# SyncE takes over 71 gathered rows of a deformable convolution, fetching each position by itself

## The chip, the core and the metric

The kernel runs on one core of one Trainium2 chip. The metric is device time in microseconds (us) of one execution. The engines are TensorE (PE; its weight loads are PEld), VectorE (DVE), ScalarE (ACT), GpSimd (POOL) and SyncE (SP); sixteen DMA engines move data between HBM and the on-chip memory.

## The reference, cut to what matters

The input x is (4, 128, 128, 128): four images, 128 channels, 128 x 128 pixels. Layer 0 is a deformable 3 x 3 convolution and a mixture of 8 experts; layer 1 is a Fourier mixing and a routed network of 64 experts. The change lies in the sampling of the deformable convolution:

```python
offset = _offset_conv(x, w_off)
...
py = base_y.astype(x.dtype)[None] + dy
px = base_x.astype(x.dtype)[None] + dx
sampled = _bilinear_gather(x, py, px)
O = w_conv.shape[0]
return jnp.einsum('bckhw,ock->bohw', sampled, w_conv.reshape(O, C, K * K))
```

For each output pixel and each of the nine taps k, a position is computed from the data, the four pixels around it are read over all 128 channels, weighted bilinearly and summed. Everything after it (the expert layer, the mixing, the routing) is done per group of image rows as soon as its nine taps are there.

## The kernel before, in words

**Tables.** Each image is normalised and written to HBM as a table of 129 x 130 entries of 256 floats: an entry holds a pixel and the pixel below it. Two entries in a row, 2 KB, are the four corners of one position. `positions` (line 649) computes for each pixel and tap the entry's number into `im.index` (128 partitions = the x of the pixel, then y, then tap) and the four corner weights.

**Chunks.** An image's 128 rows are worked in 32 groups of four rows (`row_groups`, line 162), and a group in nine chunks, one per tap; 4 x 288 = 1152 chunks in all. For one chunk (class `Chunk`, line 751):
- `gather` issues four indirect DMAs on GpSimd, one for each image row: each reads 128 positions of 2 KB, one into each partition, into a quarter of the tile g (six such tiles).
- `weighted` multiplies three of the rows by their weights on VectorE; `weighted_too` does the fourth row on ScalarE, four instructions (in a group's first chunk, tap 0, VectorE does all four rows).
- `summed` transposes and adds the four corners on TensorE, 16 matmuls into the bank trg.
- `moved` copies the result to sT on ScalarE, and `convolved` multiplies it by the weights of its tap, into sums.

**Order.** Every instruction is issued in an order written by hand (the helper at line 104, which is why most of the profile stands on L104). Time is counted in turns, two half-chunks to a chunk: the main loop makes for step n the weighting of chunk n+1, the sums of chunk n, the move of chunk n-1, and then issues the gathers of a chunk `AHEAD` = 6 steps further on (`in_turn`, line 1587). Between these, small jobs written as generators (tables of the next image, the expert layer of the last group, routing) take their turns. An engine's instructions run in that order, and an instruction that waits holds up all behind it on its engine.

**SyncE** issues the plain DMAs in the same hand-written order: loads of image blocks (xc), stores of table blocks (table<-ent), loads of the rows of a group (xg), stores of layer 1's input (x_d), expert weights and, at the end, the output. Each of its DMAs counts on one of eight completion counters, used in turn, so a DMA waits for the one issued eight before it.

**Pads.** Four padded tiles, pads 0 to 3 (line 332), hold blocks of four image rows with a zero border, for the offset convolution: `padding` (line 456) fills them on ScalarE and `offsets` (line 465) reads them in matmuls. A block uses two, and successive blocks alternate between the pairs. Late in the kernel all four serve as rooms for expert weights (`flat_pads`, line 335; `rooms`, line 1652).

**Stages.** First the table of image 0 (no gathers yet); then the sampling of all images, with the next image's table made beside it and, in the last image, the routed experts of the first three; then an ending for the last image's experts. `turns.hop` is 1 in the first and last stage and 3 during sampling.

Of the kernel before, what the change touches and what calls it, by code (L numbers as in the profile page):

```python
# [42 lines left out]
F32 = mybir.dt.float32  # L43
I32 = mybir.dt.int32
U32 = mybir.dt.uint32
AF = mybir.ActivationFunctionType
ALU = mybir.AluOpType
AX = mybir.AxisListType
# [3 lines left out]
P = 128  # L52
# [5 lines left out]
HID = 512  # L58
# [6 lines left out]
TAPS = 9  # L65
EPS_C = 1e-6
EPS_T = 1e-5
RB = 8
CB = 16
TW = P + 1  # L70
TC = P + 2
# [14 lines left out]
BANKS = 6  # L86
AFTER = 11
SPACE = 13
BLOCK = 84
FILL = "fill"  # L90
DONE = "done"
# [98 lines left out]
def metaformer_kernel(  # L190
# [50 lines left out]
    with ExitStack() as main:  # L241
# [91 lines left out]
        for pad in pads:  # L333
            nc.vector.memset(pad, 0.0)
        flat_pads = [pad.rearrange("p y x -> p (y x)")[:, 0:HID].unsqueeze(1) for pad in pads]
        aT_sb = wts.tile([P, P], F32, name="aT_sb")

        gwT_sb = wts.tile([P, 2 * E1], F32, name="gwT_sb")
# [126 lines left out]
        def offsets(im, t, padded):  # L465
# [8 lines left out]
            for k in range(3):  # L474
                for h in range(2):
                    eng.tensor.matmul(
                        po[h * P // 2 : (h + 1) * P // 2],
                        lhsT=woff_sb[:, k, :],
                        rhs=pads[(2 * t + h) % 4][:, :, k : k + P],
                        start=(k == 0),  # L480
                        stop=(k == 2),
                    )
# [268 lines left out]
        class Chunk:  # L751


            def __init__(self, group, k):
                self.group, self.k = group, k
                self.shared = k > 0

            def gather(self):
                self.g = pg.tile([P, 4, 4, P], F32, name="g", tag="g")
                im = self.group.im  # L760
                for s, y in enumerate(self.group.rows):
                    eng.gpsimd.indirect_dma_start(
                        out=self.g[:, s].rearrange("p v c -> p (v c)"),
                        out_offset=None,
                        in_=im.table,
                        in_offset=bass.IndirectOffsetOnAxis(
                            ap=im.index[:, y, self.k : self.k + 1], axis=0
                        ),
                    )

            def weighted(self):
                n = 3 if self.shared else 4
# [4 lines left out]
                )  # L777

            def weighted_too(self):
                g, y = self.g[:, 3], self.group.rows[3]  # L780
                w = self.group.im.weight[y // CB]
                for v in range(4):
                    eng.scalar.activation(
                        g[:, v, :], g[:, v, :], AF.Copy, scale=w[:, y % CB, self.k, v : v + 1]
                    )

            def summed(self):

                self.tr = bank([P, 4, P], "trg")
                for s in range(4):  # L790
                    for v in range(4):
                        eng.tensor.matmul(
                            self.tr[:, s, :],
                            lhsT=self.g[:, s, v, :],
                            rhs=ident,
                            is_transpose=True,
                            start=(v == 0),
                            stop=(v == 3),
                        )

            def moved(self):
# [2 lines left out]
                eng.scalar.copy(group.sT[self.k], self.tr)  # L804
                turns.start(group.convolved(self.k))


        exps = []

# [776 lines left out]

        def in_turn():

            for b in range(NB):
                for number, (rows_of, minus, runs) in enumerate(orders[b]):  # L1590
                    im = images[b]
                    if im.sent <= P // RB or not im.weight.keys() >= {y // CB for y in rows_of}:
                        raise ValueError("a table is late")
                    group = Group(images[b], number, rows_of, minus, runs)
                    group.begin()
                    for k in range(TAPS):
                        chunk = Chunk(group, k)
                        chunk.gather()
                        yield chunk

        source = in_turn()
        chunk = [next(source) for _ in range(AHEAD)]
        turns.hop = HOP
# [14 lines left out]
        while n < total + 3 or turns.jobs:  # L1618
# [134 lines left out]
```

## Time and profile before

| | |
|---|---|
| three runs, median | 6126.47 us (6125.08 to 6129.46) |
| the profiled execution | 6137.75 us, its span 6135.8 us |
| granted TensorE clock, mean | 0.953 |
| indirect DMAs for the tables | 4608, 3.8 us from issue to landing at the median |
| first and last of them start | 120.9 us, 5932.9 us |
| HBM read, written | 1381.43 MB, 136.85 MB |
| software queue (the gathers) | 64.9% of the sixteen DMA engines' time |
| SyncE's queue | 14.1% of it |

The page gives each engine's busy time as a share of the span, then groups of instructions by line, engine and operation with the idle time before them and what ended it ("issue": nothing that the profile shows was waited for). SyncE's instructions only issue, wait or set registers, so it has no busy share; its queue is asked for by tile.

### The profile page before, as it was taken

Reading aid. Unit: us, or ns where it says so; the run is one execution under the profiler, and the core shown is the slowest. Engines: PE = TensorE matmul, PEld = TensorE weight load, DVE = VectorE, ACT = ScalarE, POOL = GpSimd, SP = SyncE. Lnnn points to the kernel's source line nnn. Section 1 sums busy time; section 2 is a strip of 40 time slices with the busy share of each in tenths; the row PEclk is TensorE's granted clock in tenths of the full one; section 3 lists DMA queues with packets and bytes.
Section 4 is the critical chain, followed back from the end, with each engine's and each line's share of the span. In section 5 each row is a group of like instructions: output and inputs, shape, how many; then the busy total and the mean of one; then the engine's idle time right before and its main releaser. Section 6 shows DMA issues by size and latency. Waiting matters only on the chain.

```text
span 6135.8 us, 103694 instructions
## 1 busy us (share of the span) xinstructions
PE 5429.9 (88%) x31399; PEld 3754.5 (61%) x31399; DVE 4849.1 (79%) x15411; ACT 3880.8 (63%) x10047; POOL 4477.5 (73%) x4801
## 2 busy tenths in 40 slices
PE   6889999998899999998899999898888998999884
PEld 3566666666656666666666666666655665666653
DVE  5688888887788888887778888888788777788872
ACT  4567667675666766666666676666655665666662
POOL 5777777777777777777777777777777777777750
PEclk8999999999999999999999999999999999999996
DMA  7778787877777777877777778778777897999777
GB/s 233 227 238 252 243 253 240 254 236 224 240 241 243 244 244 246 246 237 221 235 245 244 245 237 248 241 237 252 221 226 215 291 337 216 328 336 318 223 221 269
DMA packets 579180, 1525.24 MB, mean 249 GB/s; under 512 B 86456, under 2 KB 225408, under 8 KB 578624
## 3 DMA queue, kind: packets, MB, share of 16 engines
q0 software_dynamic: 369664, 1210.35, 64.9%
q1 hardware_dynamic: 206656, 299.87, 14.1%
q10 hardware_dynamic: 2304, 8.39, 0.3%
q8 instruction: 253, 4.15, 0.3%
q14 instruction: 303, 2.48, 0.1%
HBM read 1381.43 MB, written 136.85 MB: 247 GB/s over the span
## 4 chain that ended last, share of the span: by engine, by line
DMA 26%; PE 25%; DVE 21%; issue 10%; POOL 9%; ACT 9%; DVEq 0%; POOLq 0%; ACTq 0%; SPq 0%
DMA g<-table,index 24%; POOL g L104 9%; PE trg L104 8%; DVE x L104 7%; DVE g L104 7%; PE sums L104 6%; PE pe L104 4%; ACT g L104 3%; PE po L104 2%; PE tr L104 2%; ACT xn L104 1%; ACT L104 1%; ACT sT L104 1%; PE small L104 1%; DVE a_st L104 1%
## 5 line engine op out<-in xcount | busy, mean ns | idle before, releaser
L104 POOL DMA_INDIRECT g<-table,index x4608 | 4375.2, 949 | 1413.2 <-issue 977.9
L104 DVE TENSOR_TENSOR g<-g,small 128x1536 f32<-128x1536 f32 (+1 forms) x1152 | 2082.6, 1808 | 827.5 <-DMA g<-table,index 762.8
L104 PEld LDWEIGHTS trg<-ident,g 128*128 128x128 f32 x18432 | 2113.8, 143 | 679.5 <-issue 458.4
L104 PE MATMUL trg<-ident,g 128*128 128x128 f32 x18432 | 2251.1, 276 | 120.7 <-DVE g L104 51.5
L104 ACT ACTIVATE g<-g,weight 128x128 f32<-128x128 f32 x4096 | 1305.9, 391 | 820.0 <-DMA g<-table,index 811.2
L104 DVE SCALAR_TENSOR_TENSOR x<-pe,gate,x 128x128 f32<-128x128 f32 x4064 | 1381.5, 342 | 97.9 <-PE pe L104 43.8
L104 PE MATMUL sums<-sT,wconv_sb 128*128 128x512 f32 x2304 | 1209.8, 626 | 42.2 <-ACT sT L104 41.5
L104 PE MATMUL pe<-ew_sb,nT 128*128 128x512 f32 x2048 | 1042.8, 607 | 76.6 <-ACT sT L104 42.1
L104 PEld LDWEIGHTS sums<-sT,wconv_sb 128*128 128x128 f32 x2304 | 437.4, 202 | 520.2 <-issue 431.8
L104 ACT COPY sT<-trg 128x512 f32<-128x512 f32 x1152 | 654.5, 568 | 135.9 <-PE trg L104 134.9
L104 PEld LDWEIGHTS pe<-ew_sb,nT 128*128 128x128 f32 x2048 | 328.9, 193 | 242.4 <-issue 104.1
L104 ACT ACT_TABLE_LOAD x264 | 338.7, 1283 | 13.5 <-DVE nmax L104 8.1
L104 ACT ACTIVATE tn<-x,d_nb,d_rs 128x128 f32<-128x128 f32 x512 | 210.9, 483 | 199.0 <-DVE d_nb L104 198.7
L104 ACT ACTIVATE c_rs<-c_mv,eps_c 128x4 f32<-128x4 f32 x128 | 38.1, 297 | 359.3 <-DVE c_mv L104 325.6
L104 ACT ACTIVATE n<-x,b_nb,b_rs 128x128 f32<-128x128 f32 x512 | 210.2, 481 | 83.6 <-DVE b_nb L104 72.1
L104 PE MATMUL tr<-ident,whole 128*128 128x128 f32 x512 | 92.2, 308 | 165.3 <-ACT whole L104 158.4
L104 ACT ACTIVATE xn<-x,c_nb,c_rs 128x128 f32<-128x128 f32 x512 | 211.3, 487 | 9.5 <-DVE c_nb L104 7.6
L104 PE MATMUL po<-pad,woff_sb 128*64 128x512 f32 x768 | 214.6, 678 | 1.9 <-ACT pad L104 1.8
L104 PE MATMUL small<-rw_sb,nT 128*128 128x8 f32 x1024 | 137.6, 261 | 85.7 <-DVE g L104 83.5
L104 PEld LDWEIGHTS small<-rw_sb,nT 128*128 128x128 f32 x1024 | 134.0, 203 | 104.0 <-DVE g L104 81.8
L104 PEld LDWEIGHTS tr<-ident,whole 128*128 128x128 f32 x512 | 61.0, 152 | 194.1 <-ACT whole L104 182.4
L104 ACT ACTIVATE ent<-raw,a_nb,a_rs 128x128 f32<-128x128 f32 x384 | 157.7, 483 | 30.9 <-DVE a_nb L104 30.1
(236 smaller groups left out, 5268.5 us busy)
## 6 DMA issues: line engine op xcount, KB each, us to landing
g<-table,index POOLq DMA_INDIRECT x4608, 3.8
table<-ent SPq DMA_DIRECT2D x48, 1024.0 KB, 6.3
xc<-in_x SPq DMA_DIRECT2D x64, 512.0 KB, 7.3
w<-x_d SPq DMA_DIRECT2D x64, 512.0 KB, 6.0
xg<-in_x SPq DMA_DIRECT2D x124, 256.0 KB, 7.3
x_d<-x SPq DMA_DIRECT2D x124, 256.0 KB, 4.0
out<-w SPq DMA_DIRECT2D x48, 512.0 KB, 4.6
w<-in_weight SPq DMA_DIRECT2D x42, 512.0 KB, 9.0
```

Source lines behind the costliest of these rows:

```text
L104: return self.tc.keep_in_program_order(issue(*args, **kwargs))
```

## The change

A new class `Lone` fetches some rows without GpSimd. Every 16 chunks it picks one chunk that is not of tap 0 (71 in the built program, none in the first 20 chunks or so) and takes its fourth image row out of the gather (`Chunk.gather` skips s = 3). For such a row:
- VectorE multiplies the row's 128 entry numbers by 1024, which makes them byte offsets into the table (an entry is 1 KB).
- SyncE stores these 128 numbers to HBM (found) and, seven turns later, loads them back as 4 partitions x 32 (places).
- During the next 26 of 32 turns, SyncE loads 16 numbers at a time into registers (eight loads of 16) and issues 128 DMAs of 2 KB, one for each position, each from the table at a register's byte offset into one partition of a flattened pad tile: five to a turn. Rows alternate between pads 2 and 3.
- The row is weighted by ScalarE and transposed by TensorE as before, but from the pad tile (`Chunk.last`).

In the built program a position is one DMA of [1, 2048] bytes without further instructions, and the queue of SyncE goes from 687 DMAs to 9917, with 568 register loads and 247 more waits for semaphores. GpSimd issues 4537 gathers instead of 4608.

Pads 2 and 3 are therefore taken from the offset convolution during sampling: `pad_of` gives both halves of every block the pads 0 and 1, and `padding` waits until `offsets` of the block before has issued its matmuls (`busy`). In the middle weight rooms, pads 2 and 3 are replaced by two tiles of the pool of corner weights.

```diff
+RUN = 16
...
+        apart = [
+            pad.rearrange("p y x -> p (y x)")[:, 0:HID].rearrange("p (v c) -> p v c", c=P)
+            for pad in pads[2:]
+        ]
+        busy = [False, False]
+        places = [wts.tile([4, P // 4], I32, name=f"places{i}") for i in range(2)]
+        scaled = [wts.tile([P, 1], I32, name=f"scaled{i}") for i in range(2)]
...
+        def pad_of(t, h):
+            return pads[(2 * t + h) % 4 if turns.hop == 1 else h]
+
         def padding(t, h, row, read, padded):
 
+            while turns.hop > 1 and busy[h]:
+                yield 1
+            busy[h] = True
             yield FILL
...
-            eng.scalar.copy(pads[(2 * t + h) % 4][:, :, 1 : P + 1], tr)
+            eng.scalar.copy(pad_of(t, h)[:, :, 1 : P + 1], tr)
...
+            busy[:] = [False, False]
             yield turns.hop
             os = pa.tile([P, 4, P], F32, name="os", tag="os", bufs=1)
...
                 for s, y in enumerate(self.group.rows):
+                    if s == 3 and self.lone is not None:
+                        continue
                     eng.gpsimd.indirect_dma_start(
...
+            def look(self, t):
+
+                i, begin = len(self.users), max(t + 16, self.end)
+                n = (begin + 2 * RUN + 9) // 2 + 1
+                n += n % TAPS == 0
...
+                self.end = begin + 2 * RUN
+                self.ahead = self.job(i, n, im, im.index[:, y, k : k + 1], begin)
+
+            def job(self, i, n, im, index, begin):
+                row = self.found[i]
+                eng.vector.tensor_scalar(scaled[i % 2], index, 8.0 * P, None, ALU.mult)
+                yield
+                yield
+                eng.sync.dma_start(out=row.unsqueeze(1), in_=scaled[i % 2])
+                for _ in range(7):
+                    yield
+                eng.sync.dma_start(out=places[i % 2], in_=row.rearrange("(a c) -> a c", a=4))
+                while self.now < begin:
+                    yield
+                self.filling, self.ahead = self.ahead, None
+                flat = im.table.rearrange("e c -> (e c)").bitcast(U8)
+                values = []
+                for p in range(P):
+                    if p % 16 == 0:
+                        a, c = divmod(p, P // 4)
+                        loads, values = nc.values_load_multi_w_load_instructions(
+                            places[i % 2][a : a + 1, c : c + 16],
+                            engines=[mybir.EngineType.SP],
+                            min_val=0,
+                            max_val=8 * P * (TW * TC - 2),
+                            skip_runtime_bounds_check_because="positions are clamped to the table",
+                        )
+                        for load in loads:
+                            tc.keep_in_program_order(load)
+                    eng.sync.dma_start(
+                        out=apart[i % 2][p : p + 1]
+                        .rearrange("p (h v) c -> p h (v c)", h=2)
+                        .bitcast(U8),
+                        in_=flat[bass.ds(values[p % 16], 16 * P)]
+                        .rearrange("(o h c) -> o h c", o=1, h=2),
+                    )
+                    if p % (P // (2 * RUN) + 1) == P // (2 * RUN):
+                        yield
...
             if 0 <= n < total:
                 chunk[n].summed()
                 turns.fill()
+                lone.turn(2 * n)
             tick(False)
...
             turns.steps()
+            if 0 <= n < total:
+                lone.turn(2 * n + 1)
...
-                rooms = [[part(), part()], [part(), part()], flat_pads]
+                rooms = [[part(), part()], [part(), part()], flat_pads[0:2]]
+                rooms[-1] += [spare(), spare()]
```

More of the change, by code (lines that the diff above doesn't have):

```diff
@@ L45 @@
 U32 = mybir.dt.uint32
+U8 = mybir.dt.uint8
 AF = mybir.ActivationFunctionType
@@ L478, in offsets @@
                         lhsT=woff_sb[:, k, :],
-                        rhs=pads[(2 * t + h) % 4][:, :, k : k + P],
+                        rhs=pad_of(t, h)[:, :, k : k + P],
                         start=(k == 0),
@@ L756, in __init__ @@
                 self.shared = k > 0
+                self.lone = None
             def gather(self):
@@ L769, in gather, with last @@
                     )
+            def last(self):
+                return self.g[:, 3] if self.lone is None else self.lone
             def weighted(self):
@@ L779, in weighted_too @@
             def weighted_too(self):
-                g, y = self.g[:, 3], self.group.rows[3]
+                g, y = self.last(), self.group.rows[3]
                 w = self.group.im.weight[y // CB]
@@ L790, in summed @@
                 for s in range(4):
+                    g = self.g[:, s] if s < 3 else self.last()
                     for v in range(4):
@@ L793, in summed @@
                             self.tr[:, s, :],
-                            lhsT=self.g[:, s, v, :],
+                            lhsT=g[:, v, :],
                             rhs=ident,
@@ L805, in moved, with __init__, turn @@
                 turns.start(group.convolved(self.k))
+        class Lone:
+            def __init__(self):
+                self.found = dram.tile([total // RUN + 2, P], I32, name="found")
+                self.tiles, self.users, self.end = {}, [], 0
+                self.ahead = self.filling = None
+                self.values = []
+            def look(self, t):
+                i, begin = len(self.users), max(t + 16, self.end)
+                n = (begin + 2 * RUN + 9) // 2 + 1
+                n += n % TAPS == 0
+                b, k = divmod(n, slots)
+                number, k = divmod(k, TAPS)
+                if n >= total or b not in images or i > 1 and begin <= 2 * self.users[-2]:
+                    return
+                im, y = images[b], orders[b][number][0][3]
+                if im.sent <= P // RB or im.known <= y // CB:
+                    return
+                self.users.append(n)
+                self.tiles[n] = apart[i % 2]
+                self.end = begin + 2 * RUN
[35 more added lines that the diff above has]
+                        yield
+                if self.now >= 2 * n - 2:
+                    raise ValueError("a row is late")
+            def turn(self, t):
+                self.now = t
+                if self.filling is not None and next(self.filling, DONE) is DONE:
+                    self.filling = None
+                if self.ahead is None:
+                    self.look(t)
+                if self.ahead is not None:
+                    next(self.ahead)
@@ L1587, in in_turn @@
         def in_turn():
+            n = 0
             for b in range(NB):
@@ L1597, in in_turn @@
                         chunk = Chunk(group, k)
+                        chunk.lone = lone.tiles.get(n)
+                        n += 1
                         chunk.gather()
                         yield chunk
+        lone = Lone()
         source = in_turn()
@@ L1650, in metaformer_kernel @@
                 part = lambda: late.tile([P, 2, HID], F32, name="w", tag="w", bufs=4)
-                rooms = [[part(), part()], [part(), part()], flat_pads]
+                spare = lambda: pw.tile(
+                    [P, 1, HID], F32, name="w", tag="weight", bufs=3 * P // CB // 2
+                )
+                rooms = [[part(), part()], [part(), part()], flat_pads[0:2]]
+                rooms[-1] += [spare(), spare()]
                 rooms.append([pw.tile([P, 2, HID], F32, name="w", tag="index")])
```

## The prediction

> **What bounds the kernel now.** I read the page's busy shares first, then its costliest groups, then the order of time on GpSimd, then the table of waits, then busy time by stretch, and last the two tables on SyncE's own instructions. The busy shares alone mislead:
>
> ```profile
> PE 5429.9 (88%) x31399; PEld 3754.5 (61%) x31399; DVE 4849.1 (79%) x15411; ACT 3880.8 (63%) x10047; POOL 4477.5 (73%) x4801
> ```
>
> TensorE looks like the bound and GpSimd (POOL) like an engine with a quarter of its time free. The group of the gathers and GpSimd's order of time say otherwise:
>
> ```profile
> L104 POOL DMA_INDIRECT g<-table,index x4608 | 4375.2, 949 | 1413.2 <-issue 977.9
> ```
> ```profile
> 2301.55 0.95 POOL L104 DMA_INDIRECT g<-table,index  x1 [0.30 <-issue]
> 2302.80 0.94 POOL L104 DMA_INDIRECT g<-table,index  x1 [0.30 <-issue]
> 2304.04 0.95 POOL L104 DMA_INDIRECT g<-table,index  x1 [0.30 <-issue]
> ```
>
> The 1413 us of "idle" are 4608 gaps of 0.30 us, and the gaps come whatever else happens: a gather costs 1.254 us from start to start (median of all of them). 4608 x 1.254 = 5778 us, and the first gather starts at 120.9 us, the last at 5932.9: 5812 us. So GpSimd issues back to back all through the sampling; only some 34 us of it are anything else (most of that the 24 indirect DMAs of the experts, 24 x 1.254 = 30 us). The other engines wait for it:
>
> ```profile
> POOL g L104 <- issue: 977.9, 3208, 0.3
> ACT g L104 <- DMA g<-table,index: 811.2, 403, 19.2
> DVE g L104 <- DMA g<-table,index: 762.8, 465, 15.2
> ```
> ```profile
> 1000.00:2000.00 1000.00, 911.43 (x5100) 625.63 (x5099) 824.32 (x2671) 667.00 (x1739) 757.05 (x798) 0.96 0.79 240
> 3000.00:4000.00 1000.00, 913.00 (x5135) 625.14 (x5135) 824.18 (x2667) 676.79 (x1762) 757.06 (x798) 0.97 0.80 243
> 5000.00:5934.00 934.00, 848.93 (x5076) 609.03 (x5073) 746.75 (x2173) 578.00 (x1489) 705.03 (x744) 0.96 0.85 280
> ```
>
> In the first fence the third column is the longest single wait: GpSimd's never passes 0.3 us, those of ScalarE and VectorE for a gather reach 15 to 19. In the second, columns are PE, PEld, DVE, ACT, POOL, clock, DMA share. The fullest engine, TensorE, is 91% busy where a chunk takes 4 x 1.254 = 5.02 us: 4.58 us of work, so chunks could come every 4.6 us before it decides.
>
> **What is removed.** 71 chunks issue three gathers instead of four: 71 x 1.254 = **89.0 us** off the engine that sets the pace. The saving is spread, one gather in every 16 chunks, so the mean chunk goes from 5.02 to 4.94 us, above TensorE's 4.58. Consumers already wait 763 and 811 us, so they follow. Nothing else on GpSimd grows.
>
> **What is added, off the path.** VectorE gets 71 scalings of a 128x1 column. The nearest small one in the trace (128x8, 163 ns) makes 71 x 0.16 = 12 us in 5812, below its 763 us of waiting; if that cover were gone, 12 us. The transposes and ScalarE weightings of the moved row are the same in number and only read another tile. Halving the pads makes a block's second padding wait for the offset matmuls of the block before. Blocks come some 30 turns apart (75 us) and use their pads for about ten, so I cost it at nothing; without that cover a table would come late and GpSimd itself would wait. Three expert weight rooms become four smaller ones at the same bytes: nothing.
>
> **What decides: SyncE.** A row is now 128 DMAs of 2 KB on the SyncE queue, 71 x 128 = 9088 in all, beside 8 register loads, one store and one load of its indices. Rows start 32 half-chunk turns apart, 16 x 5.02 = 80.3 us, so SyncE must do a row in that time. What is the cost of one?
>
> ```profile
> L104 SPq DMA_DIRECT2D table<-ent x51: 332/366/372, 401.3 to 4233.0; - x51
> L104 SPq DMA_DIRECT2D table<-zeros x8: 462/596/709, 2.8 to 3005.9; - x8
> L104 SPq DMA_DIRECT2D xc<-table x5: 413/462/870, 118.2 to 193.1; - x5
> ```
>
> (Min/median/max ns of one issue.) Issues stand 0.05 us apart. Bounds: 0.32 us (shortest issue of the queue) + 0.05 = 0.37, and 0.60 + 0.05 = 0.65 for the table<-zeros median. Four of those eight move only two runs of 1 KB, in shape the nearest to the new DMA, and took 0.58 to 0.70. But the built program carries a mark on every other DMA of this queue, the 9088 new ones included, that these four lack, and the marked sibling just before each took 0.46 to 0.47 (0.71 at the kernel's start). So I go by marked rows: 0.366 when alone, 0.43 right behind another; with 0.05 between, and a register for the address, **0.46 us**: 128 x 0.46 = 59 us.
>
> A register load is not in the trace. Below: 0.02 us (a bare semaphore wait of SyncE, 17 ns); above: 2.8 us (a DMA's full round trip: the median gather's 3.8 less the 0.95 in which GpSimd issues it). I take 0.5, nearer to an issue, since it moves 64 bytes: 8 x 0.5 = 4 us (0.2 to 22). Other work per row: two index DMAs at 0.42, 0.8 us; of the 551 DMAs SyncE issues between 121 and 5934 us, 551/72 x 0.42 = 3.2 us; and 2 us for small DMAs queued behind a 1 MB table store. Sum 59 + 4 + 6 = **69 us of 80.3** (low 47 + 0 + 4 = 51, high 83 + 22 + 6 = 111).
>
> The eight completion counters of the queue add a limit: in the built program each DMA waits for the one issued eight before it. A landing of L us gives at best L/8 per DMA. Rows: 3.1 us (shortest x_d store in the sampling), 3.8 us (median gather, 0.95 of it GpSimd's), 4.8 us (a 0.2 KB load behind megabytes at the start), 7.3 (256 KB load). A 2 KB read resembles a gather less its issue, 2.8 us, plus 0.4 of its own: 3.2/8 = 0.40, under 0.46. Behind the waiting DMA stand the x_d stores and xg loads; they would be late by a few us, and xg is fetched six chunks (30 us) ahead.
>
> **The skill.** The trace shows no register load, so I set a rule against mine: the Trainium skill, Runtime: NRT & Kernel Launch, section "Instruction fetch mechanics", puts such loads at about 200 ns per register even in bulk. By it 16 registers would take 3.2 us, a row's eight loads 26 us, and the row 91 us: slower than the gathers. It speaks of registers from HBM; these come from SBUF, and no row here shows either.
>
> DMA engines: the share of 0.79 to 0.85 is the mean over sixteen. The Trainium skill, DMA: Bandwidth & Descriptors, section "Why a DMA increments its semaphore by 16 and not by 1", says that a DMA spreads over as many engines as divide its slowest dimension, the lowest-numbered ones; by it a single 2 KB run may sit on one engine always. No row here shows engines apart. I bound the cost without it: spread evenly the new packets are 9088 x 0.09 us / 16 = 51 us per engine, less than the gathers' removed; all on one engine, 9088 x (0.090 + 0.009) = 0.90 ms on top of 0.797 x 6136 = 4.89 ms, less 0.06: 5.73 ms in 6.05 (2 KB packets of queue 1 average 90 ns and semaphore packets 9 ns in the packet records). Full, not over; only the last stretch (0.85 x 934 + 145 = 939 in 920) could lose some 15 us.
>
> **The sum.** The profiled execution took 6137.75 us (span 6135.8), 11.3 above the median of 6126.47; the saving is the same in both: 6137.75 - 89.0 = 6048.75, or 6126.5 - 89.0 = 6037.5. I add 3 us for later landings at the end of the sampling (3.8 us at the median, up to 9.8 seen): **6040 us**. What is late next is GpSimd again, at 4537 gathers.
>
> **Rivals.** Under 0.2% (12 us) cannot be told from no change.
> 1. *SyncE cannot keep up* (slower). Place: the row's last position lands after ScalarE wants it; the chain waits on the pad tile, and GpSimd stalls on buffers. It decides once a position costs over (80.3 - 10)/128 = 0.55 us, whether by issue or by a landing over 4.4 us. Price: 71 x (128 p + 10 - 79.1), measured from 6040: p = 0.58 gives 6420, the table<-zeros figure 0.65 gives 7046. For it: the two-run rows at 0.58 to 0.70. Against: the mark, and 0.366 for a whole 1 MB store.
> 2. *One DMA engine fills up* and stretches the gathers; part of the gain goes: 6060 to 6115, and beyond 6.5% stretch it is slower too (5.73 x 1.10 = 6.30 ms).
> 3. *The gain does not appear*: another engine paces by 5 us a chunk anyway, 6126. Against: 4.58 us of TensorE work.
>
> **How the numbers follow.** Forecast 0.58 (own range 6030 to 6060); rival 2 with part of the gain 0.09, slower 0.05; rival 1 slower 0.25; rival 3 0.03. Faster 0.58 + 0.09 = 0.67, same 0.03, slower 0.30. The range runs from 6028 up into rival 1 as far as p = 0.58, 6420, leaving out its dearer half and a little below.
>
> **What would show it.** Right: 4537 gathers still 1.254 us apart and the last one near 5844 us; SyncE issues of 0.4 to 0.5 us; no long waits of ScalarE on the pad tiles. Wrong: gathers with gaps over 0.3 us waiting for PE or ACT, ScalarE's g waits naming a SyncE DMA, SyncE issuing without pause. A gather's landing well over 3.8 us with GpSimd still back to back would speak for rival 2 without a loss.

## The result, and the profile after

The changed kernel takes **6330.9 us** (median of six runs, 6323.7 to 6343.7) against 6127.3 us for the kernel before, run in turn with it: ratio 1.0333, interval 1.0319 to 1.0346. The forecast was 6040 us; the change makes the kernel 3.3% slower. The profiled execution took 6343.73 us, 12.8 above the median; its span is 6341.6 us, the granted clock 0.934.

Of the nine groups of experiments below, six met the chip in a condition in which the kernel before itself takes 7302 to 7387 us (clock 0.89); each ratio is taken within its group, and the readings rest on the groups at 6126 to 6140 us unless the text says otherwise.

The page's busy shares and its group of the gathers (mean ns, then idle time before them and what ended it):

```profile
PE 5472.2 (86%) x31399; PEld 3804.0 (60%) x31399; DVE 4836.4 (76%) x15482; ACT 3877.7 (61%) x10047; POOL 4400.7 (69%) x4730
...
L106 POOL DMA_INDIRECT g<-table,index x4537 | 4298.8, 947 | 1690.2 <-issue 1029.3
```

71 gathers are gone and each still takes 947 ns, but the idle time before them rose from 1413 to 1690 us. The table of waits (total, times, longest) says why. The first line is the kernel before, the others are the changed kernel:

```profile
POOL g L104 <- DMA g<-table,index: 118.0, 387, 0.3
...
POOL g L106 <- issue: 1029.3, 3226, 9.7
DVE g L106 <- DMA g<-table,index: 629.7, 251, 15.0
ACT g L106 <- DMA g<-table,index: 605.2, 210, 19.1
POOL g L106 <- DMA g<-table,index: 184.2, 288, 4.1
```

The first and the last line belong together: a gather that waits for a gather. In the kernel before such a wait fits into the gap of 0.3 us that stands before every gather; now it is up to 4.1 us long. By stretch (same columns as before, PE to DMA share):

```profile
1000.00:2000.00 1000.00, 896.49 (x5080) 624.25 (x5078) 816.91 (x2655) 657.71 (x1720) 740.73 (x782) 0.96 0.83 238
3000.00:4000.00 1000.00, 905.02 (x5079) 626.04 (x5078) 812.39 (x2652) 666.53 (x1739) 738.28 (x780) 0.95 0.84 241
5000.00:5934.00 934.00, 759.37 (x4638) 545.77 (x4637) 625.66 (x1839) 492.67 (x1259) 585.74 (x619) 0.90 0.83 256
```

In the first two, GpSimd made 782 and 780 indirect DMAs in 1000 us instead of 798. With one gather in 64 taken away it should have made as many and finished more chunks; it made fewer. In the last stretch it made 619 instead of 744, and every engine is emptier: the fullest, TensorE, is 81% busy there.

Where the time went can be read by stage. Each chunk ends in one ScalarE copy (sT from trg); its start times, taken from the trace's records, split the span (us; the first 864 chunks are images 0 to 2):

| kernel | first 864 chunks end (the 865th copy starts) | last image's 288 | rest | span |
|---|---|---|---|---|
| before | 4477.7 | 1466.3 | 191.8 | 6135.8 |
| after | 4512.0 | 1633.9 | 195.7 | 6341.6 |
| indices by TensorE, all rows | 4404.5 | 1549.2 | 191.6 | 6145.3 |
| indices by TensorE, rows in images 0 to 2 only | 4403.8 | 1463.2 | 191.8 | 6058.8 |

So there are two losses: 34 us instead of a gain of some 70 in the first three images, and 168 us in the last one. The first comes from the store of the indices; of the second about half goes with that store and half stays without it.

### The profile page after: what moved, and what is told of

Same layout as the page of the kernel before. It is cut to its first block, busy times and chain, and to the rows that moved or that the text cites. A ratio compares the mean times of both kernels' runs of the same rounds, so it can differ in the third digit from the quotient of the medians.

```text
span 6341.6 us, 122668 instructions
## 1 busy us (share of the span) xinstructions
PE 5472.2 (86%) x31399; PEld 3804.0 (60%) x31399; DVE 4836.4 (76%) x15482; ACT 3877.7 (61%) x10047; POOL 4400.7 (69%) x4730
## 4 chain that ended last, share of the span: by engine, by line
PE 31%; DMA 27%; DVE 17%; issue 9%; ACT 8%; POOL 6%; SPq 2%; DVEq 0%; ACTq 0%; POOLq 0%; another core or an unknown queue 0%
DMA g<-table,index 17%; PE trg L106 10%; PE sums L106 8%; PE pe L106 6%; POOL g L106 6%; DVE x L106 5%; DVE g L106 5%; PE tr L106 2%; PE po L106 2%; ACT g L106 2%; DMA pad<-table 2%; DMA out<-w 2%; DMA w<-in_weight 2%; SPq L106 2%; DMA w<-x_d 2%
## 5 line engine op out<-in xcount | busy, mean ns | idle before, releaser
L106 POOL DMA_INDIRECT g<-table,index x4537 | 4298.8, 947 | 1690.2 <-issue 1029.3
L106 ACT ACTIVATE g<-g,weight 128x128 f32<-128x128 f32 x3812 | 1215.4, 392 | 662.5 <-DMA g<-table,index 605.2
L106 PE MATMUL po<-pad,woff_sb 128*64 128x512 f32 x768 | 197.5, 627 | 2.2 <-ACT pad L106 2.2
L106 DVE MAX8 best<-lq 128x8 f32<-128x256 f32 (+2 forms) x256 | 106.5, 416 | 83.7 <-ACT lq L106 83.1
L106 ACT COPY w<-pf 128x512 f32<-128x512 f32 x64 | 37.0, 584 | 213.2 <-DMA out<-w 146.3
```

The lines of the kernel that those rows point to most:

```text
L106: return self.tc.keep_in_program_order(issue(*args, **kwargs))
```

## The first three images: a store of 512 bytes

SyncE does what was forecast, and better. Its issues by tile (min/median/max ns):

```profile
L106 SPq DMA_DIRECT2D pad<-table x9088: 9/228/2047, 149.3 to 6090.2; - x198
L875 SPq TENSOR_LOAD <-places x568: 1132/1240/4518, 148.0 to 6083.3; - x190
L106 SPq DMA_DIRECT2D found<-scaled x71: 327/366/369, 133.6 to 5964.3; - x71
```

A position is one run (one contiguous piece) of 2 KB; its issue takes 228 ns, the move of its register 29 ns, and from start to start it is 0.323 us at the median (0.51 at the mean up to 4400 us, gaps over 3 us left out). Up to 5300 us ScalarE waited 0.8 us in all for a row read in this way. But about once per row GpSimd stops. One such stop, in order of time, first SyncE and then GpSimd (start, us, operation, idle before it and what ended it):

```profile
2368.54 0.37 SPq L106 DMA_DIRECT2D found<-scaled  x1
2369.01 21.89 SPq L106 DMA_DIRECT2D pad<-table  x30
```
```profile
2376.70 0.94 POOL L106 DMA_INDIRECT g<-table,index  x1 [0.30 <-ACT a_rs L106]
2377.95 0.95 POOL L106 DMA_INDIRECT g<-table,index  x1 [0.30 <-issue]
2382.32 0.94 POOL L106 DMA_INDIRECT g<-table,index  x1 [3.43 <-DMA g<-table,index]
```

At 2368.5 SyncE stores the 128 scaled indices, 128 pieces of 4 bytes. Some ten microseconds later a gather waits 3.4 us. In the records the gather it waits for is the one eight before it (issued at 2369.2, landed at 2382.1): GpSimd's DMAs too count on eight completion counters used in turn, so a gather can start only when the one eight before has landed. Eight gathers take 8 x 1.254 = 10.0 us; a landing up to that costs nothing, one above it stops GpSimd. The landings (issue to last of 16 increments), sorted by the time since the last store, all up to 4400 us:

| issued after the store | after: gathers, median us | store alone, no reads (five runs): gathers, us |
|---|---|---|
| 0 to 3 us | 122, 10.8 | 7, 9.2 to 13.5 |
| 3 to 6 us | 130, 10.1 | 2, 9.1 and 9.3 |
| 6 to 9 us | 129, 8.9 | 1, 6.7 |
| 12 to 15 us | 96, 5.4 | 9, medians 3.6 to 5.1 |
| 20 to 30 us | 418, 4.0 | 56, medians 3.5 to 3.7 |

Every gather issued in the nine microseconds after a store takes over 6 us, 381 of 381. The trace's packet records show the same from the side of the DMA engines. They hold every 4 KB packet of the gathers with its time (packets started per us, then mean ns of one; stores between 300 and 4400 us):

| us from the store | after, 51 stores | store alone, four runs, 168 stores |
|---|---|---|
| -6 to 0 | 52, 215 | 40, 221 |
| 2 to 4 | 27, 1075 | 18, 1084 |
| 4 to 6 | 8, 1354 | 8, 1255 |
| 6 to 8 | 10, 886 | 9, 915 |
| 8 to 10 | 11, 558 | 13, 447 |
| 10 to 12 | 50, 204 | 53, 197 |

The store's own packets of 4 bytes take 9 ns each. But from the second to the tenth microsecond after it a gather's packets take two and a half to six times as long, and a half to a sixth as many start; SyncE's 1 KB packets go from 46 to 51 ns up to 208 to 254 (third to fifth microsecond). In the kernel before and in the run with reads and no store (below), packets looked at every 80 us take 211 to 221 ns throughout. The reload comes some 25 us after the store, when landings are normal again, so it is the store and not the reload. Beyond 0.3 us GpSimd lost 108.8 us in 90 stops in these images; 89 of them, 107.9 us, lie within 20 us after one of the 54 stores: 2.0 us for each. The account closes: by the end of the first 864 chunks GpSimd has issued 55 DMAs fewer, 55 x 1.254 = 69.0 us gained, and has lost 104.6 us (all spacings against 1.254, taken together); net 36 against the 34 measured.

**Experiment: the indices by another way (all rows kept).** TensorE transposes the 128 numbers into one PSUM row and VectorE copies them to one partition, where the registers are loaded from; neither store nor load is left. (Two small tiles of constants move into a shared room to make space.)

```diff
-                eng.sync.dma_start(out=row.unsqueeze(1), in_=scaled[i % 2])
-                eng.sync.dma_start(out=places[i % 2], in_=row.rearrange("(a c) -> a c", a=4))
+                tr = bank([P, P], "along")
+                eng.tensor.transpose(tr[0:1, :], scaled[i % 2], ident)
+                eng.vector.tensor_copy(places[i % 2], tr[0:1, :])
```

> The same kernel as e3_indices_by_tensore, on another chip: on the chip of the first four runs the kernel before itself took 7376 us in place of 6127 and GpSimd was held up in most chunks by TensorE, so that nothing there speaks of a kernel that GpSimd paces. Where the kernel before takes 6127 us: theory (the sparse store of the 128 numbers holds up the gathers) 6230 us or below, the first 864 chunks at 4.95 us each; rival (the position fetches hold them up) 6330 us and gathers that still land late once a row.

Measured: 6147.5 us, ratio 1.0034 (1.0022 to 1.0045) in a group at 6130; the theory's 6230 or below is met, the rival's 6330 is not. GpSimd's waits up to 4500 us, first the changed kernel, then this one:

```profile
POOL g L106 <- issue: 741.9, 2416, 2.1
POOL g L106 <- DMA g<-table,index: 147.1, 230, 4.1
```
```profile
POOL g L106 <- issue: 771.4, 2531, 0.3
POOL g L106 <- DMA g<-table,index: 55.2, 181, 0.3
```

Not one such stop is left, and the first 864 chunks end 73 us ahead of before (4404.5 against 4477.7): 52 DMAs fewer at 1.254 are 65 us, and the rest is that the profiled executions space them by 1.252 us at the mean here and by 1.254 before. The 107.5 us between this run and the changed kernel there go with the store and its reload, and by the landings and packets above with the store. The reads themselves, 2 KB each on SyncE's queue beside the gathers, cost GpSimd nothing: no stop, and packets of the old length.

**Experiment: the store alone (indices scaled, stored and loaded; no reads, all 4608 gathers kept).** The `for p in range(P)` loop loses its register loads and DMAs, and no row leaves the gather.

It ran four times, with these expectations in order:

> Every row stays with GpSimd; SyncE only stores the 128 numbers of 4 bytes to HBM and loads them back, 71 times; no position is fetched and no register loaded, and the moved row is not taken from the gather. Theory (the sparse store holds up the DMA engines, so that gathers behind it land at 11 us in place of 3.7 and GpSimd, whose gather waits for the one eight before, stalls some 2 us a row): 6127 + 71 x 1.9 = 6260 us, with a stall of GpSimd at nearly every store. Rival (the position fetches crowd the engines): 6127 us, no stalls.

> The kernel of the indices-only run again: each row's indices are scaled, stored to HBM as 128 numbers of 4 bytes and read back, but no row is read by SyncE and GpSimd keeps all 4608 gathers. Theory (the store of 4-byte pieces makes gathers land late for some 15 us, and GpSimd stalls because a gather waits for the one eight before it): one stall of 1 to 3 us at each of the 71 stores, nothing to pay for it, so 6127 + 71 x 1.5 to 2.5 us = 6230 to 6300. Rival (the late landings need the positions' own traffic or SyncE's full queue as well): 6127 to 6150.

> Again the kernel that only scales, stores and reloads the indices, with all 4608 gathers on GpSimd and no reads by SyncE. Theory (the store of 128 pieces of 4 bytes alone makes the gathers around it land late, and each waits for the one eight before): a stall of 1.5 to 2.5 us at each of 71 stores, 6230 to 6300. Rival (late landings need SyncE's reads as well): 6127 to 6150.

> Only the indices' scaling, store and reload, all 4608 gathers on GpSimd, no reads by SyncE; for a chip where the kernel before takes about 6130. Theory (the store of 128 pieces of 4 bytes alone makes gathers around it land late, and each waits for the one eight before): a stall of 1.5 to 2.5 us at each of 71 stores, 6230 to 6300. Rival (late landings need SyncE's reads as well): 6127 to 6150.

All four fell in groups in which chunks come every 6.05 us: 7412.5 against 7376.0 (1.005), 7313.7 against 7310.0 (1.0009, interval 0.9996 to 1.0022), 7412.7 against 7387.4 (1.0048) and 7334.0 against 7305.0 (1.0039). There GpSimd has 1 us to spare per chunk, so the price could not show, and the expected 6230 to 6300 was neither met nor refuted. The landings could: few of those gathers have all increments on record, but in the right column above all nine that were issued within 6 us of a store took 9 to 13 us, and the packet records show the slow packets at these stores as in the changed kernel. The late landings come from the store by itself; SyncE's reads are not needed for them.

The store itself is slow: 8.8 us from issue to its last increment (median of 67), where the 512 KB stores of the output take 4.8. The Trainium skill, DMA: Bandwidth & Descriptors, section "Specifications", says that transfers below 512 bytes are done as read-modify-write. A piece of 4 bytes is far below; the runs agree that it is dear, but no run shows the mechanism, nor why the packets of other DMAs slow down for it.

**Experiment: pads alone.** No row is ever picked (`if True or n >= total ...`); two pads for the blocks, the `busy` wait and the smaller weight rooms stay.

> No row is moved: only the halved pads, the busy gate and the smaller weight rooms are left of the change. The theory (the loss comes from what SyncE does for a row) expects the time of before, 6127 us within 10. The rival that the pads and rooms cost the time expects up to 6330. Pace of the first 864 chunks: 5.02 us by both but the rival.

Measured: 7373.3 against 7376.0, ratio 1.000 (0.9989 to 1.0012). The rearranged pads and rooms cost nothing, though this group hides what less than GpSimd's slack would cost; the best version below, which keeps them and gains 63 us of 66, bounds it where GpSimd sets the pace.

## The last image: SyncE's queue carries more than the reads

Without the store the last image still takes 1549 us instead of 1466, and it has 18 gathers fewer.

**Experiment: rows in images 0 to 2 only (indices by TensorE).**

```diff
-                if n >= total or b not in images or ...
+                if n >= LATE * slots or b not in images or ...
```

> Two edits together: the indices go to SyncE by TensorE and VectorE with no store to HBM and no load of it, and no chunk of the last image gives up a gather (rows only in the first three images, 53 or so instead of 71). Theory (store slows the gathers' landings; what is left is lost only where SyncE's queue also carries the experts' weights and the output): chunks 0 to 864 at 4.94 us as in the run with indices by TensorE and rows everywhere, 73 us gained, and the last image at the old 1466 us: 6054 to 6062, faster than before by 1.1 to 1.2%. Rival (the last image loses by the four smaller expert weight rooms or the two pads, not by SyncE's rows): the last image still takes some 1550 us, in all about 6140. Rival 2 (GpSimd's gain is lost in another way as soon as the tail begins): 6100.

> The kernel with indices by TensorE and rows in the first three images only, once more, on a chip where the kernel before takes about 6130. Theory (the store of 4-byte pieces slows gathers; what is then left is lost only in the last image, where SyncE's queue also carries the experts' weights and the output): 54 rows or so, chunks 0 to 864 gain 73 us, the last image takes its old 1466 us: 6054 to 6062. Rival (the last image loses by the smaller weight rooms or the two pads): last image about 1550, in all 6140.

> Indices by TensorE, rows in the first three images only, a third time, for a chip where the kernel before takes about 6130. Theory (the store of 4-byte pieces costs the first three images their gain; what is lost after that is lost only where SyncE's queue also carries the experts' weights and the output): chunks 0 to 864 gain 73 us, the last image takes its old 1466 us: 6054 to 6062, ratio 0.989. Rival (the last image loses by the smaller weight rooms or the two pads): last image about 1550, in all 6140, ratio 1.002. Where the kernel before takes some 7300 to 7400 us, TensorE sets the pace, and the ratio is again about 1.016 to 1.019.

The first two fell in groups at 7310 and 7387 us: 7419.2 us, ratio 1.0155 (1.0137 to 1.0174), and 7517.5 us, 1.0186 (1.0165 to 1.0206). The third: **6063.3 us** against 6126.1, ratio 0.990 (0.9884 to 0.9917), 1% below the kernel before: 53 gathers less, 66 us by 1.254, of which 63 are measured. The last image takes 1463.2 us, the old time, so its loss comes from SyncE's rows in it and not from pads or rooms.

How do reads that are never late lose time? The waits from 4540 to 5950 us, for the kernel before, for the run with all rows, and for this one:

```profile
POOL g L104 <- issue: 234.4, 769, 0.3
ACT w L104 <- DMA out<-w: 28.7, 8, 7.3
DVE w L104 <- DMA out<-w: 4.6, 5, 1.1
```
```profile
ACT w L106 <- DMA out<-w: 88.9, 18, 12.9
DVE w L106 <- DMA out<-w: 66.9, 13, 11.3
POOL g L106 <- ACT sT L106: 56.2, 28, 12.6
```
```profile
ACT w L106 <- DMA out<-w: 31.0, 10, 6.5
POOL g L106 <- ACT sT L106: 6.4, 21, 0.3
DVE w L106 <- DMA out<-w: 6.3, 5, 2.1
```

In the last image the output of the first three is turned and stored too: ScalarE and VectorE copy into a room w, SyncE stores it (out), and the next copy into that room waits for the store. From the trace's records, for the 48 such stores of SyncE: the store is issued 0.1 us after its two copies have ended in the kernel before (median; 0.2 at the 90th percentile), 0.1 (0.1) with rows in images 0 to 2, but 10.9 (17.7) with all rows, and 13.0 (20.5) in the changed kernel. The stores stand behind reads. So rooms come free late, ScalarE and VectorE wait 156 us for them instead of 33, and because they work in order the copies sT wait behind, the tiles g come free late, and GpSimd stops for up to 12.6 us. And why the queue is full, by SyncE's own waits between 5000 and 5720 us (before, then all rows by TensorE):

```profile
SPq L104 <- DVE w L104: 273.4, 45, 16.0
SPq L104 <- DVE x L104: 152.6, 7, 47.0
```
```profile
SPq L106 <- DMA w<-x_d: 71.2, 38, 3.6
SPq L106 <- DVE w L106: 28.9, 5, 9.5
SPq L106 <- DMA out<-w: 27.2, 25, 3.7
SPq L106 <- DMA pad<-table: 16.9, 43, 1.4
```

Before, SyncE waits for its producers (VectorE's copies), which is slack. Now it waits for landings, and the producers wait for it. A row took 91 us there at the median (86 at the mean) from first load to first load of the next, against 80 us (79) in the first three images.

**Experiment: SyncE's time without reads (failed).** In the last image GpSimd was to gather all rows while SyncE made 40 register loads per row.

> Indices by TensorE, rows in the first three images as in the run with indices by TensorE. In the last image GpSimd gathers all four rows of every chunk again, and SyncE issues none of the 128 small reads of a row, but keeps some 50 us of its time per row busy with register loads alone (40 loads of 16 registers instead of 8 loads and 128 positions); these take no DMA engine and no completion counter. The loaded numbers are used by nothing. Theory (SyncE's time and order hold back the loads and stores of the last image, and the in-order engines behind them): the last image takes about 1466 + 83 = 1550 us plus up to 22 us for the 18 gathers put back, so 6140 to 6170 in all, with long waits of ScalarE and VectorE for the output's stores. Rival (the small reads hurt as traffic, or by holding the queue's eight completion counters): the last image keeps 1466 us and the whole is 6055 to 6065.

> Again the kernel whose last image has 40 register loads per row on SyncE, some 50 us of its time, instead of the reads of a row (GpSimd gathers all four rows there). Theory (SyncE's time and order hold up the loads and stores of the last image): the last image takes 1550 us or more, 6140 to 6170 in all. Rival (the small reads hurt as traffic or by holding the queue's eight completion counters): the last image keeps 1466 us, 6055 to 6065 in all.

> As the run with indices by TensorE and rows in the first three images only (6063 us), but in the last image SyncE is kept busy some 50 us per row by 40 register loads that nothing uses; GpSimd gathers every row there, and no small read is issued. For a chip where the kernel before takes about 6130. Theory (SyncE's time and order hold up the loads and stores of the last image): the last image takes 1550 us or so, 6140 to 6165 in all, with long waits of ScalarE and VectorE for the output's stores. Rival (the small reads hurt as traffic or by holding the queue's eight completion counters): the last image keeps 1463 us, 6060 to 6070 in all. In between: both. Where the kernel before takes 7300 us or more, the run says little of either.

> Rows in the first three images only, indices by TensorE, and 40 register loads per row on SyncE in the last image in place of the reads. Seen on two chips where the kernel before takes 7300 us or more, the last image takes as long as without the loads (within 9 us). Theory now (the small reads themselves, by their counters and their place in the queue, hold up the last image): also where the kernel before takes 6130 the last image keeps 1463 us, 6060 to 6070 in all, ratio 0.989 to 0.991. Rival (SyncE's bare time does it): the last image 1550 us, 6140 to 6165, ratio 1.002 to 1.006.

Measured in the fourth: 6077.8 against 6139.7 us, ratio 0.9899 (0.9883 to 0.9916), and 1.0159, 1.0196 and 1.0173 in the others, in groups at 7310, 7387 and 7305, as the kernel without any loads there. That looks like the verdict "SyncE's time is free". But the trace has no register load at all after 4332 us: nothing used the loaded numbers, and the built program is without these loads. What ran is the kernel with rows in three images plus the last image's transposes and some 700 semaphore instructions of SyncE, which cost little (last image 1470.8 us). The question it was to answer stays open, and what the fourth expectation says of the earlier runs is no evidence either.

**Experiment: short reads in the last image.** GpSimd gathers all rows there and SyncE issues a row's 128 reads of two runs of 32 bytes, which nothing uses.

> Rows in the first three images as in the run with indices by TensorE and early rows (6063 us). In the last image GpSimd gathers all four rows of every chunk, and SyncE issues a row's 128 reads all the same, with their register loads, but each of two runs of 32 bytes instead of two of 1 KB; nothing uses what they bring. Theory (a read takes a completion counter of SyncE's queue, so each read waits for the DMA eight before it, often a 512 KB load or store of the last image, and the stores and loads stand behind the reads): the last image takes some 1549 us and up to 22 more for the 18 gathers put back, 6140 to 6170 in all, ratio 1.002 to 1.007, with waits of ScalarE and VectorE for the output's stores as in the run with all rows. Rival (the traffic of the 2 KB packets): the last image keeps 1463 us, 6060 to 6075, ratio 0.989 to 0.991. Where the kernel before takes 7300 us or more, the run says little.

Measured: 7973.3 against 7301.7 us, ratio 1.0915 (1.0894 to 1.0936). The last image took 2334 us against 1778 to 1821 without reads in such groups, and the issue itself had changed (the same kernel, in images 0 to 2 with reads of one run of 2 KB and from 5000 us on with two runs of 32 bytes):

```profile
L106 SPq DMA_DIRECT2D pad<-table x4424: 2/228/1416, 999.9 to 4398.3; - x193
...
L106 SPq DMA_DIRECT2D pad<-table x2764: 2/562/1620, 5000.4 to 7699.9; - x198
```

The recorded expectation takes the reads of 2 KB for two runs of 1 KB; in the trace each is one run. An issue of two 32-byte runs takes 562 ns, not 228, so this kernel does not hold SyncE's time fixed and cannot tell traffic from counters. (The two-run rows that the prediction showed, table<-zeros with runs of 1 KB, took 584 to 702 ns, which fits the number of runs rather than the bytes as the reason; no run separates the two.) A position then takes 0.87 us at the mean, 128 of them 111 us, more than sixteen chunks last. It does show that reads whose data nobody needs can cost over 500 us, and the loads behind them are late: TensorE waited up to 55 us for a load w<-x_d and up to 38 us for xg.

**Experiment: two halves.** Images 0 to 2 with the store and without reads; the last image with all reads, indices by TensorE, and the output's stores issued on ScalarE's queue.

```diff
-                    (eng.sync if self.among else eng.scalar).dma_start(
+                    (eng.sync if self.among and turns.hop == 1 else eng.scalar).dma_start(
```

> Two questions in two stages of one kernel. First three images: the indices are scaled, stored to HBM as 128 numbers of 4 bytes and read back as in the changed kernel, but no row is read by SyncE and GpSimd keeps all its gathers. Last image: indices by TensorE, rows read by SyncE as in the run with indices by TensorE everywhere, but the output's stores (out from w) of that image are issued on ScalarE's queue instead of SyncE's. Nothing is left out of the result. Stage one (chunks 0 to 864; 4338 us before, 4365 in the changed kernel, 4266 with indices by TensorE): theory (the store by itself makes gathers land late, each waits for the one eight before): 54 stalls of 1 to 2.5 us, 4390 to 4470 us; rival (late landings need SyncE's reads as well): 4338 to 4350. Stage two (chunks 864 to 1151; 1466 us before, 1549 with all rows, 1463 without rows): theory (the stores and what waits for them stand behind reads that wait for their counters): most of the 83 us come back, 1470 to 1500; rival (the loads of weights behind the reads, or the reads' counters alone): 1530 to 1560, or more where ScalarE waits in its own order. Where the kernel before takes 7300 us or more, the run says little of either.

Measured: 7374.1 against 7303.3 us, ratio 1.0102 (1.0084 to 1.0121), in a group that says nothing of the first half. The last image took 1833.6 us; with the stores on SyncE it took 1886.4 and without rows 1788.4, in other groups of this kind. ScalarE's and VectorE's waits for the output's stores in the last image, with the stores on SyncE's queue and on ScalarE's:

```profile
ACT w L106 <- DMA out<-w: 70.9, 15, 12.8
DVE w L106 <- DMA out<-w: 54.7, 12, 11.7
```
```profile
ACT w L106 <- DMA out<-w: 13.2, 3, 6.7
DVE w L106 <- DMA out<-w: 3.2, 1, 3.2
```

Most of these waits are gone and about half of the loss with them. That fits the stores' place in the queue as one part and the loads behind the reads as the other; across groups, and where GpSimd does not set the pace, it is a hint and not proof.

**The other runs.** In the first group (7376 us) the kernel with indices by TensorE took 7598.7 (1.0298, interval 1.0261 to 1.0334), and the one that keeps the store but has rows only in images 0 to 2 took 7640.2 (1.036):

> As the changed kernel, but the 128 numbers come to one partition by a transpose on TensorE and a copy on VectorE; no store to HBM and no load back. Theory: the first 864 chunks come at 4.95 us in place of 5.05, about 100 us off, and SyncE, which no longer waits 5.6 us a row for that store, holds up the last image less: 6230 us or below. Rival (the position fetches): 6330 us as before, gathers still landing late once a row.

> Rows are moved in the first three images only, 54 or so in place of 71; the store to HBM stays. Theory (in the last image SyncE's queue, which also carries the expert weights and the output, is too full, and its late loads and stores hold up the other engines; some 166 us of the loss arise there): the last image runs as before, 6127 + 34 = 6161 us. Rival (the last image is slow by the same stalls as the others, one store a row): the loss goes down only by 17 rows of 71, to about 6280.

Neither number was met, since GpSimd was not the bound. Their first 864 chunks, 5387 and 5501 us after chunk 0, differ by 114 us, again in favour of the kernel without the store. A row every 13 chunks instead of 16 (RUN = 13), rows in three images:

> As the kernel with indices by TensorE and rows in the first three images only, but a row every 13 chunks instead of 16, some 66 rows. A row takes SyncE 41 us of issues, 10 of register loads and 5 of other work, 56 us of 13 x 4.94 = 64. Theory: another 12 x 1.25 = 15 us off GpSimd, 6040 to 6048. Rival (SyncE has too little slack, rows or table loads come late, or chunks come nearer to TensorE's 4.6 us and its jitter shows): 6055 or more.

Measured: 7902.3 against 7387.4 us, ratio 1.0702 (1.0684 to 1.072). ScalarE's longest kinds of wait:

```profile
ACT sT L106 <- remote: 651.3, 175, 15.7
ACT pad L106 <- DMA pad<-table: 519.1, 48, 25.8
```

Here the rows are late, which is the prediction's rival 1. The mean position takes 0.67 us from start to start in this run and 0.74 to 0.76 in the others of these groups with reads of 2 KB, instead of 0.48 (gaps over 3 us left out; one in five to one in four is over 1.3). That is past the 0.55 us from which the prediction had that rival decide, and a row of 13 chunks has 87 us here, little more than the 80.3 that the condition was worked out for. The gain of the best version, 1%, therefore belongs to the groups at 6126 to 6140 us, where GpSimd sets the pace; in the others it loses 1.6 to 1.9%.

## Why the prediction was wrong, point by point

1. **GpSimd is the bound.** Right for the kernel before and still right in images 0 to 2: where nothing stops it the new kernel's gathers are 1.25 us apart. That GpSimd's waits "never pass 0.3 us" holds for its waits for an earlier gather and for "issue", not for all of its waits in the kernel before (1.9 us once in the last image); it changes nothing in the sum.
2. **71 x 1.254 = 89.0 us, consumers follow.** Right in size where it was set free: the best version has 53 gathers less, 66 us, and gains 63. In the last image it never appeared.
3. **Pads, rooms, VectorE's scalings at nothing.** Held: the best version contains them all and lacks 3 us of its 66.
4. **SyncE's row at 69 us.** A position was put at 0.46 us; it is 0.323 at the median and 0.51 at the mean, waits included. A register load was put at 0.5 us and is 1.24. SyncE's account of a mean row in the changed kernel, from the records: 31 us of issues, 4 of moves, 11 of register loads, 10 of short gaps, 4 of other DMAs, and 24 of waits (5.8 for the landing of the store of indices, 4.6 for VectorE's scaling), 84 in all. Its work was less than forecast; waits filled the rest. Without the store, too, some 21 us of a row in images 0 to 2 are waits, then mostly for VectorE and ScalarE.
5. **The two index DMAs, "0.42 each, 0.8 us" of SyncE's time. This is the step that failed.** It priced the store as an issue and never asked what 128 pieces of 4 bytes do to the DMAs beside it. The store makes every gather of the next nine microseconds land late, at a median of 9 to 11 us instead of 3.8, and there GpSimd's own eight counters bite: 2.0 us per row against the 1.254 saved. Set against the run without it, the store's path costs 107 us in images 0 to 2, 85 in the last one and 4 in the rest: 196 us between the profiled executions, 183 between the medians (6330.9 and 6147.5, in groups at 6127.3 and 6130.0). (How the 85 divide between late gathers and SyncE's waits is not shown.) The prediction had worked the rule of eight counters for SyncE (landing / 8) and not for the engine that it had named as the bound, where the same division gives 10.0 us of landing as the point at which it starts to pay.
6. **The last image was not costed by itself.** This is a second, smaller step that failed. The row's time was held against 80.3 us everywhere, with the queue's other DMAs spread evenly (551 in the sampling). In the last image they crowd: stores of 512 KB and loads stand among the reads, and the output's stores are issued 10.9 us late at the median, not "a few us". That is 83 us, on top of the gain of 18 gathers that did not appear, 23 us. With the store's 183 the miss closes: 183 + 83 + 23 = 289 of the 291 us between 6040 and 6330.9.
7. **Rivals.** The time lay inside the range, but by none of its cases, so that is luck. Rival 1's late rows did not occur in the changed kernel (0.8 us of waits; its mean position, 0.52 us over the whole kernel, stays just under the 0.55 of the condition); they did where a position took 0.67 us. Its prices are also off by a few us: the formula as printed gives 6405 for 0.58 and 7041 for 0.65, not 6420 and 7046. Rival 2 named gathers that land later, by a DMA engine that fills. The reads alone have a little of that: without the store the gathers up to 4400 us land at 4.00 us at the median instead of 3.78 (the 15th of the 16 increments at 3.74 instead of 3.66), and it costs nothing, since GpSimd has 10.0. The late landings that did cost came from the store, in short spells. Rival 3 is excluded by the best version.
8. **The skill's rule on registers.** The Trainium skill, Runtime: NRT & Kernel Launch, section "Instruction fetch mechanics", has about 200 ns per register, 3.2 us for 16. Measured here from SBUF: 1.24 us for 16, 78 ns each. The measurement decides for loads from SBUF; no run here shows one from HBM.

What stays open: why the packets of other DMAs slow down after the small store; how the last image's 83 us divide between SyncE's bare time, its reads' counters and their traffic; and what the 1.6 to 1.9% are that the best version loses in the groups at 7302 us and more.

## What to carry to other kernels

Before work is moved to a queue, price the small DMAs that feed it by what they do to the bound's own DMAs, and not only by their issue: find the number of DMAs that the bound may have under way, multiply by their spacing, and ask whether anything can push a landing past that. Move a column of numbers across partitions by TensorE and VectorE rather than by a store of single words to HBM and back. And cost a queue's new load in the stage where it is fullest, by who waits for the DMA behind it.

## What the runs showed of the hardware that was not expected

- A store of 128 x 4 bytes to HBM takes 8.8 us to land, and gathers issued up to 9 us after it land at a median of 9 to 11 us instead of 3.8. Its own packets take 9 ns each; what slows are the packets of the other DMAs, the 4 KB ones from 215 ns to 1354 at the mean between 4 and 6 us after it.
- SyncE issues a DMA with a register address in 228 ns when it is one run of 2 KB, but in 562 ns with two runs of 32 bytes (medians).
- A load of 16 registers from SBUF holds SyncE for 1.24 us at the median (1.13 to 4.5).
